# The first loads in one queue, and a second sequence's slots beside the first one's dense mixture

## The chip, the cores and the metric

The kernel runs on one core of a Trainium2 chip. The core has five engines with a sequencer each: PE (matrix products and transposes; PEld is its weight load), DVE, ACT and POOL (element-wise work, POOL also gathers rows by index), and SP, which only issues DMAs. Sixteen DMA engines move data between memory and the on-chip buffers. The metric is the device time of one execution in microseconds (us); less is better. A change of about 0.5% is what runs of this kernel can tell from none.

## The reference, cut to what matters

Eight sequences of 1024 rows of 256 numbers go through three residual blocks: a mixture of experts, an attention block, and the same mixture of experts again.

```python
x = x + 0.5 * ffn(layernorm(x))
x = x + attention(layernorm(x))
x = x + 0.5 * ffn(layernorm(x))

def ffn(y):              # 8 experts of width 128, two of them for each row
    w = softmax(y @ router_w + router_b); keep the two largest, scaled to sum 1
    out = sum over experts e of  w[e] * (gelu(y @ W1[e] + b1[e]) @ W2[e] + b2[e])

def attention(x):
    light: 8 heads of 64 in windows of 64 rows, each with the window before and after
    heavy: two router scores per row; the 256 best rows by each, full attention between them,
           added to the light result at the rows chosen
```

## The kernel before

**Two ways to do a mixture.** Sequence 0's first mixture and sequence 7's last one are *dense* (`dense`): all eight experts for every row, in groups of rows. Per expert, PE makes `ph` (rows turned, 512 columns, two products), ACT takes a Gelu into `act`, PE makes `po` for four tiles of 128 rows, and DVE adds `po` times a row's weight to the rows (`x_0at<-po_0f,weight_0f`, four sums per expert and half). The turned and normalised rows lie in a tile `yTf`. Sequence 0 goes in two halves of four tiles. All other mixtures are *routed*. `rows` normalises a sequence's rows, stores them to memory (`y_1f<-rows_1f`), takes the router's logits (`pl`), ranks the experts (`better`), and gives each pair of row and expert a slot in an order sorted by expert, padded to 128 (`slot`, `at`, and through `who` the `token` of every slot). `experts` then goes through 23 blocks of 128 slots: POOL gathers the rows (`xp`), SP fetches the block's expert, 256.5 KB (`wt<-wpk`, the number read from `te_i`), PE turns the rows (`pt`), makes `ph` and `po`, and the result goes to memory (`ys`). `combine` later gathers a row's two results (`got`) and adds them.

**Packed weights.** `wpk` is a table in memory with one row of w1, w2 and b1 for each expert and partition. Four copies from memory to memory make it at the start; every fetch of `wt` reads it.

**Attention.** `front(b)` adds the gathered results to sequence b's rows (for sequence 0 the dense mixture has done it in place), stores them (`h_a`), normalises, turns them (`xT`), and takes two scores a row (`junk`, `sc`). The scores are turned by PE (`pr`), sent to memory as a line and read back to all partitions (`line`, `rbuf`), and compared with each row's own (`cmp`, 46 DVE steps per sequence) for a `rank`, from which the 256 best rows follow. `project` makes q, k and v into `qT`, `kT` and `v`; `light` and `heavy` are the two attentions.

**What sets the order.** The functions above are generators. They are advanced in the order of a list of stages, `sides`, each with a number of steps and a start and end on an axis on which one sequence is 1 long. An operation is then only recorded. A planner (`Plan`) takes all recorded operations, their data dependencies and the reuse of buffers, estimates costs, and lays out each engine's queue; it does this some rounds, keeps the best by its own estimate, and emits the instructions in that order. An engine runs its queue strictly in order. The recording order decides which buffer of a tag an operation gets, and so which earlier users it must wait for; PSUM banks (three for general use) are given out by the planner. The field `behind` ties an operation to an earlier one in the plan.

**The start.** `nc.sync.dma_start` stands in SP's queue, `nc.scalar.dma_start` in ACT's. In this kernel SP loads all eight tiles of sequence 0's rows in one DMA (1 MB) and then sequence 1's rows. ACT issues the rest: all experts for the dense mixture in two DMAs of 1 MB (`all_experts`), the router, the four copies to `wpk`, the small b2, and the nine attention weights (`attention_loads`); an issuing instruction takes its place in ACT's order among the copies and Gelus. In `sides`, the rows of sequence 1 are recorded from -1.50 to -0.98, its experts from -0.95 to 0.10, and the dense mixture of sequence 0 from -2.2 to -1.6.

Every operation is issued through a recording helper, so the profile gives line 197 for most of them; they are told apart by their tiles' names. In those, `0f` is the first mixture of sequence 0, `7f` that of the last dense one, `1at` the attention of sequence 1, `atl` light and `ath` heavy.

Of the kernel before, what the change touches and what calls it, by code (L numbers as in the profile page):

```python
# [44 lines left out]
F32 = mybir.dt.float32  # L45
# [12 lines left out]
P = 128  # L58
# [158 lines left out]
class Plan:  # L217
# [201 lines left out]
    def schedule(self, before, after, rank):  # L419
# [60 lines left out]
        while len(result) < len(ops):  # L480
            e = min((e for e in ENGINES if found[e]), key=lambda e: found[e][0])
            t, k = found[e]
            o = ops[k]
            for x in o.engines:
                waiting[x].remove((rank[k], k))
            stale = set(o.engines)
            func = o.how.get("func")
            if func in TABLES and func != table:
                t += SWITCH if table else 0
                table = func  # L490
            takes, seen_after = o.cost(e)
            if e == PE:
                changed = o.how["array"] != array
                array = o.how["array"]
                now[e] = run(t, takes + (TURN if changed else 0))
                done = now[e] + (170 if clock[0] == 1 else 230)
            else:
                now[e], done = t + takes, t + seen_after + LATE
            if o.kind == "dma":
                lane = max(t + o.how["lag"] + LATE_DMA - 200, lane) + o.how["bytes"] / RATE  # L500
                done = lane + 300
                length[k] = o.how["lag"] + LATE_DMA + o.how["bytes"] / RATE + 100
            else:
                length[k] = takes + 200 if e == PE else seen_after + LATE
            end = max(end, done)
            result.append((t, k, e))
            for i in self.opens[k]:
                asks[i] -= 1
            for i in self.uses[k]:
                if i not in bank_of:  # L510

                    bank_of[i] = max(
                        free_at,
                        key=lambda x: (free_at[x] <= t, free_at[x] if free_at[x] <= t else -free_at[x], -x),
                    )
                    del free_at[bank_of[i]]
                last_use[i] = max(last_use[i], done)
                left[i] -= 1
                if not left[i]:
                    free_at[bank_of[i]] = last_use[i]  # L520
            if self.opens[k] or self.uses[k]:
                stale.add(PE)
            for q in after[k]:
                missing[q] -= 1
                same = e == PE and ops[q].engines == (PE,)
                ready[q] = max(ready[q], now[e] - SIGNAL[e] if same else done)
                if not missing[q]:
                    for x in ops[q].engines:
                        insort(waiting[x], (rank[q], q))
                        stale.add(x)  # L530
            for x in stale:
                found[x] = next_of(x)
        return end, result, length, bank_of

    def backward(self, before, result, length, bank_of):
# [27 lines left out]
        for _ in range(n):  # L563
            e = min((e for e in ENGINES if found[e]), key=lambda e: found[e][0])
            t, k = found[e]
            waiting[e].remove((-begin[k], -k))
            now[e] = from_end[k] = t + takes[k]
            stale = {e}
            for q in before[k]:
                x = engine[q]  # L570
                if x == PE and e == PE:
                    ready[q] = max(ready[q], from_end[k] + takes[q])
                else:
                    ready[q] = max(ready[q], from_end[k] + length[q] + SIGNAL[e])
                missing[q] -= 1
                if not missing[q]:
                    insort(waiting[x], (-begin[q], -q))
                    stale.add(x)
            for x in stale:
                found[x] = next_of(x)  # L580
# [43 lines left out]
def program(  # L624
# [46 lines left out]


    x1_0 = one.tile([P, NT, D], F32, tag="x1", name="x1_0at")
    nc.sync.dma_start(out=x1_0, in_=by_tile(x, 0))
    b1_sb = load(b1, "b1_sb")

    def all_experts(queue, name):
        t = one.tile([P, 2 * E * D], F32, tag="hbuf", name=name)
        w1_of = t[:, : E * D].rearrange("p (k e h) -> p k e h", k=KD, e=E)
        w2_of = t[:, E * D :].rearrange("p (e d) -> p e d", e=E)  # L680
        queue.dma_start(out=w1_of, in_=w1)
        queue.dma_start(out=w2_of, in_=w2)
        return w1_of, w2_of

    experts_0 = all_experts(nc.scalar, "experts_0")
    rw_sb = load(router_w, "rw_sb")
    rb_sb = cons.tile([P, E], F32, tag="rb_sb", name="rb_sb")
    nc.scalar.dma_start(out=rb_sb, in_=router_b.partition_broadcast(P))
    wpk_p = wpk.rearrange("e p c -> p e c")
    for k in range(KD):  # L690
        nc.scalar.dma_start(out=wpk_p[:, :, ts(k, FE)], in_=w1[:, k, :, :])
    nc.scalar.dma_start(out=wpk_p[:, :, KD * FE : KD * FE + D], in_=w2)
    nc.scalar.dma_start(out=wpk_p[:, :, WROW - 1], in_=b1, allow_slow_non_contiguous=True)

    ident = cons.tile([P, P], F32, tag="ident", name="ident")
    make_identity(nc, ident)
# [69 lines left out]
    expert = cons.tile([96, 1], F32, tag="expert", name="expert")  # L766
    nc.gpsimd.memset(expert, -1.0)
    for i in range(3):
        nc.scalar.dma_start(out=b2_sb[32 * i : 32 * i + E, :], in_=b2)
        nc.gpsimd.iota(  # L770
            expert[32 * i : 32 * i + 32, :],
            pattern=[[0, 1]],
            base=0,
            channel_multiplier=1,
            allow_small_or_imprecise_dtypes=True,
        )

    all_sel = cons.tile([96, E], BF16, tag="all_sel", name="all_sel")
    nc.vector.tensor_scalar(all_sel, place_f[:96, :E], expert, None, op0=ALU.is_equal)
    b2_part = two.tile([P, 2 * D], BF16, tag="y", name="b2_part")[:96, :D]  # L780
    b2_s = cons.tile([96, D], BF16, tag="b2_s", name="b2_s")
    nc.vector.tensor_copy(b2_s, b2_sb)
    for i in range(1, 3):
# [104 lines left out]
    def rows(f, src, group, routed):  # L888
# [12 lines left out]
        for i_b, b in enumerate(group):  # L901
            n = f"{b}f{f}"
            y = one.tile([P, NT, D], F32, tag="rows", name=f"rows_{n}")
            nc.sync.dma_start(out=y, in_=by_tile(src, b)).waits = completed[b] if f else ()
            mv, rstd = yield from stats(y, n)
            ls = lg[:, ts(i_b, NT), :]
            for hf in range(2):
# [240 lines left out]
        nc.vector.tensor_tensor(gate[1], gate[0], ex, op=ALU.mult)  # L1148
        return gate

    def dense(rows_of, weights, n):

# [8 lines left out]
            nc.vector.bn_aggr(mv[:, i, :], st[:, i, :])  # L1163
        nc.vector.tensor_scalar_add(ve[:, :m], mv[:, :m, 1], EPS)
        nc.gpsimd.tensor_tensor(rstd[:, :m], ve[:, :m], mhalf[:, :m], op=ALU.pow)
        yT = one.tile([P, KD, HALF], F32, tag="yTf", name=f"yTf_{n}")
        for h in range(m // 2):
            pt = bank(f"pt_{n}_{h}")
            for i in range(2):
# [624 lines left out]
    def first_dense():  # L1794

        tiles = [x1_0[:, t, :] for t in range(NT)]
        for hf in range(2):
            yield from dense(tiles[4 * hf : 4 * hf + 4], experts_0, f"0f0_{hf}")

    def last_dense(c, last_weights):  # L1800

        if not last_weights:
            last_weights.extend(all_experts(nc.sync, "experts_1"))
        assert ended[0] >= 2 * c + 2
        yield from dense(last_tiles[2 * c : 2 * c + 2], last_weights, f"7f1_{c}")
        for t in (2 * c, 2 * c + 1):
# [35 lines left out]
    def attention_loads():  # L1842

        for t, src in attention_weights:
            nc.scalar.dma_start(out=t, in_=src)
        nc.vector.tensor_scalar_mul(gam16, gam_sb, D**0.5)
        yield

# [4 lines left out]
    sides = []  # L1853
    for group in FIRST:
        a, z = steps(group)
        at = group[0] - 2 + (0.05 if group[0] == 1 else 0)
        sides.append((first_rows(group), a, at - 0.55, at - 0.03))
        sides.append((first_experts(group), z, at, at + 1.05))
    for group in LAST:
# [78 lines left out]
```

## Time and profile before

| | us |
|---|---|
| median of 9 runs | 1851.34 |
| lowest and highest run | 1838.19, 1859.10 |
| the profiled execution: its time | 1845.04 |
| its span in the profile | 1843.3 |
| busy in it: PE, DVE, ACT, POOL | 1698.9, 1351.6, 925.3, 874.8 |
| first 128x512 expert product (ph_0f) starts | 28.41 |
| sequence 0's scores compared (cmp_0at) | 178.3 to 206.2 |
| second sequence's experts' first product (ph_2f) starts | 247.06 |

The profile is of one execution. Its page gives busy times, the span in 40 slices, DMA queues, the chain of work that ended last, and the costliest groups. The trace behind it can be asked for a timeline (start, duration, engine, operation, output and inputs, and in brackets how long the engine was idle before and what released it), for who waited for whom, and for sums over any stretch of time. A DMA's issue stands under the issuing engine with a q.

### The profile page before, as it was taken

Reading aid. Unit: us, or ns where it says so; the run is one execution under the profiler, and the core shown is the slowest. Engines: PE = TensorE matmul, PEld = TensorE weight load, DVE = VectorE, ACT = ScalarE, POOL = GpSimd, SP = SyncE. Lnnn points to the kernel's source line nnn. Section 1 sums busy time; section 2 is a strip of 40 time slices with the busy share of each in tenths; the row PEclk is TensorE's granted clock in tenths of the full one; section 3 lists DMA queues with packets and bytes.
Section 4 is the critical chain, followed back from the end, with each engine's and each line's share of the span. In section 5 each row is a group of like instructions: output and inputs, shape, how many; then the busy total and the mean of one; then the engine's idle time right before and its main releaser. Section 6 shows DMA issues by size and latency. Waiting matters only on the chain.

```text
span 1843.3 us, 40072 instructions
## 1 busy us (share of the span) xinstructions
PE 1698.9 (92%) x13844; PEld 1254.8 (68%) x13844; DVE 1351.6 (73%) x4303; ACT 925.3 (50%) x2568; POOL 874.8 (47%) x771
## 2 busy tenths in 40 slices
PE   4888899999999999899999999999999999899996
PEld 2555577667777677667766777767676777667774
DVE  4563967988795796988993877779774878558744
ACT  1113456545564565446553675646564565555431
POOL 1005363355344671463645555574445635555523
PEclk9988899999999999999999999999999999999998
DMA  8117456234667566245566387555565476535363
GB/s 234 24 59 242 136 178 205 71 115 138 205 220 214 154 198 193 65 138 192 184 188 186 114 255 235 176 169 179 185 197 166 134 233 202 150 109 188 116 190 107
DMA packets 223323, 306.22 MB, mean 166 GB/s; under 512 B 54648, under 2 KB 158736, under 8 KB 221328
## 3 DMA queue, kind: packets, MB, share of 16 engines
q1 hardware_dynamic: 188288, 216.81, 36.8%
q0 software_dynamic: 28608, 78.16, 15.7%
q10 hardware_dynamic: 6224, 8.70, 1.9%
q8 instruction: 109, 1.79, 0.4%
q14 instruction: 94, 0.77, 0.1%
HBM read 214.90 MB, written 83.43 MB: 162 GB/s over the span
## 4 chain that ended last, share of the span: by engine, by line
PE 48%; DVE 22%; DMA 14%; issue 9%; POOL 4%; ACT 3%; POOLq 0%; SPq 0%; ACTq 0%; DVEq 0%
PE po_0f L197 2%; PE ph_0f L197 2%; PE po_7f L197 2%; PE ph_7f L197 1%; DMA xp_5f<-y_5f,token_5f 1%; PE po_1f L197 1%; PE ph_1f L197 1%; PE po_6f L197 1%; DVE cmp_3at L197 1%; DMA wt_6f<-wpk 1%; DVE cmp_1at L197 1%; DMA xp_1f<-y_1f,token_1f 1%; DMA wpk<-in_w 1%; DVE cmp_4at L197 1%; DVE o L197 1%
## 5 line engine op out<-in xcount | busy, mean ns | idle before, releaser
L197 ACT ACT_TABLE_LOAD x93 | 119.3, 1283 | 19.2 <-DVE nmax_6atl L197 8.8
L197 POOL DMA_INDIRECT xp_1f<-y_1f,token_1f x62 | 71.0, 1145 | 72.5 <-PE pt_1f L197 21.4
L197 POOL DMA_INDIRECT xp_3f<-y_3f,token_3f x62 | 65.3, 1053 | 43.8 <-issue 13.9
L197 POOL DMA_INDIRECT xp_6f<-y_6f,token_6f x46 | 48.1, 1046 | 63.2 <-PE pt_6f L197 38.5
L197 POOL DMA_INDIRECT xp_5f<-y_5f,token_5f x46 | 48.0, 1043 | 43.8 <-PE pt_5f L197 23.9
L197 DVE SCALAR_TENSOR_TENSOR x_0at<-po_0f,weight_0f,x_0at 128x256 f32<-128x256 f32 x64 | 27.9, 478 | 39.2 <-PE po_0f L197 38.5
L197 DVE SCALAR_TENSOR_TENSOR x_last<-po_7f,weight_7f,x_last 128x256 f32<-128x256 f32 x64 | 28.2, 479 | 34.6 <-PE po_7f L197 34.4
L197 ACT ACTIVATE act_0f<-ph_0f,b_sb 128x512 f32<-128x512 f32 x16 | 11.0, 687 | 62.1 <-PE ph_0f L197 53.4
L197 PE MATMUL po_0f<-experts,act_0f 128*128 128x256 f32 x128 | 35.8, 386 | 5.3 <-ACT act_0f L197 5.3
L197 POOL DMA_INDIRECT xp_7f<-y_7f,token_7f x23 | 25.2, 1096 | 31.6 <-PE pt_3f L197 15.0
L197 PEld LDWEIGHTS ph_1f<-xTe_1f,wt_1f 128*128 128x128 f32 x248 | 34.4, 194 | 8.3 <-issue 6.6
L197 PE MATMUL ph_3f<-xTe_3f,wt_3f 128*128 128x128 f32 x248 | 37.1, 281 | 2.6 <-DMA wt_3f<-wpk 2.6
L289 POOL TENSOR_TENSOR a_3atl<-a_3atl,asum_3atl 128x768 f32<-128x768 f32 x14 | 20.7, 1481 | 37.7 <-DVE asum_3atl L197 22.9
L197 PEld LDWEIGHTS ph_3f<-xTe_3f,wt_3f 128*128 128x128 f32 x248 | 33.2, 192 | 7.9 <-DMA wt_3f<-wpk 4.5
L289 POOL TENSOR_TENSOR a_2atl<-a_2atl,asum_2atl 128x768 f32<-128x768 f32 x10 | 14.8, 1475 | 48.8 <-DVE asum_2atl L197 27.9
L197 PE MATMUL ph_0f<-yTf_0f,experts 128*128 128x512 f32 x64 | 34.2, 661 | 3.9 <-ACT act_0f L197 3.9
L197 PE MATMUL ph_1f<-xTe_1f,wt_1f 128*128 128x128 f32 x248 | 37.3, 281 | 0.0
L197 PE MATMUL ph_7f<-yTf_7f,experts 128*128 128x256 f32 x128 | 33.6, 385 | 3.6 <-ACT act_7f L197 3.6
L197 POOL DMA_INDIRECT xp_0f<-y_0f,token_0f x23 | 24.2, 1053 | 26.5 <-PE pt_0f L197 12.0
L197 ACT ACTIVATE act_7f<-ph_7f,b_sb 128x256 f32<-128x256 f32 x32 | 15.1, 473 | 42.5 <-PE ph_7f L197 30.6
L197 PE MATMUL po_7f<-experts,act_7f 128*128 128x256 f32 x128 | 36.4, 378 | 0.0
L197 PE MATMUL po_1f<-wt_1f,act_1f 128*128 128x256 f32 x124 | 35.1, 381 | 0.2 <-ACT act_1f L197 0.2
(1570 smaller groups left out, 6197.6 us busy)
## 6 DMA issues: line engine op xcount, KB each, us to landing
wt_1f<-wpk SPq DMA_DIRECT2D x62, 256.5 KB
wt_3f<-wpk SPq DMA_DIRECT2D x62, 256.5 KB
wt_5f<-wpk SPq DMA_DIRECT2D x46, 256.5 KB
wt_6f<-wpk SPq DMA_DIRECT2D x46, 256.5 KB
ys_1f<-yp_1f SPq DMA_DIRECT2D x30, 256.0 KB
ys_3f<-yp_3f SPq DMA_DIRECT2D x30, 256.0 KB
o<-h_b SPq DMA_DIRECT2D x56, 128.0 KB
out_x<-o SPq DMA_DIRECT2D x56, 128.0 KB
```

The lines of the kernel that those rows point to most:

```text
L197: op = Op(self.plan, engines, lambda _: issue(*args, **kw), outs, ins, kind, **how)
L289: return getattr(nc, engine).tensor_tensor(dst, dst, by, op=ALU.mult)
```

## The change

- The loads of the start go through `in_line` into SP's queue, one behind the other in the plan: two tiles of sequence 0's rows, two more, the first four experts in three DMAs, the other four tiles, the other four experts, sequence 1's rows, b2, the copies to `wpk`, the nine attention weights. ACT keeps b1 and the router's two.
- `all_experts` loads in six DMAs, four experts at a time, with the layout of w1 in its tile unchanged in size.
- The planner treats an operation that is `behind` a DMA as able to follow at once, without waiting for the DMA's end.
- Sequence 1's rows are recorded from -2.15 to -1.7 and its experts from -1.3 to -0.3. The first half and second half of sequence 0's turned rows lie in `qT`, so that the tile `yTf` is free for sequence 1's.
- `b2_part` takes another buffer.

The planner lays out the whole program anew, so queues differ in detail from there to the end.

```diff
@@ schedule
-                same = e == PE and ops[q].engines == (PE,)
+                same = e == PE and ops[q].engines == (PE,) or ops[q].behind is o and o.kind == "dma"
@@ backward
-                if x == PE and e == PE:
+                if x == PE and e == PE or self.ops[k].behind is self.ops[q] and self.ops[q].kind == "dma":
@@ program, the first loads
-    nc.sync.dma_start(out=x1_0, in_=by_tile(x, 0))
+    first_loads = []
+
+    def in_line(out, in_, **kw):
+
+        o = nc.sync.dma_start(out=out, in_=in_, **kw)
+        o.behind = first_loads[-1] if first_loads else None
+        first_loads.append(o)
+
+    def load_x1_0(t):
+        in_line(x1_0[:, t : t + 2, :], by_tile(x, 0)[:, t : t + 2, :])
+
+    for t in range(0, 4, 2):
+        load_x1_0(t)
     b1_sb = load(b1, "b1_sb")
-    def all_experts(queue, name):
+    def all_experts(name, dma_start, between=None):
         t = one.tile([P, 2 * E * D], F32, tag="hbuf", name=name)
-        w1_of = t[:, : E * D].rearrange("p (k e h) -> p k e h", k=KD, e=E)
-        w2_of = t[:, E * D :].rearrange("p (e d) -> p e d", e=E)
-        queue.dma_start(out=w1_of, in_=w1)
-        queue.dma_start(out=w2_of, in_=w2)
+        w1_of, w2_of = t[:, : E * D], t[:, E * D :]
+        w1_of = w1_of.rearrange("p (e k h) -> p k e h", k=KD, e=E)
+        w2_of = w2_of.rearrange("p (e d) -> p e d", e=E)
+        for e in range(0, E, 4):
+            for k in range(KD):
+                dma_start(out=w1_of[:, k, e : e + 4, :], in_=w1[:, k, e : e + 4, :])
+            dma_start(out=w2_of[:, e : e + 4, :], in_=w2[:, e : e + 4, :])
+            if between and not e:
+                for t in range(4, NT, 2):
+                    between(t)
         return w1_of, w2_of
-    experts_0 = all_experts(nc.scalar, "experts_0")
+    experts_0 = all_experts("experts_0", in_line, load_x1_0)
...
     for k in range(KD):
-        nc.scalar.dma_start(out=wpk_p[:, :, ts(k, FE)], in_=w1[:, k, :, :])
-    nc.scalar.dma_start(out=wpk_p[:, :, KD * FE : KD * FE + D], in_=w2)
-    nc.scalar.dma_start(out=wpk_p[:, :, WROW - 1], in_=b1, allow_slow_non_contiguous=True)
+        in_line(wpk_p[:, :, ts(k, FE)], w1[:, k, :, :])
+    in_line(wpk_p[:, :, KD * FE : KD * FE + D], w2)
+    in_line(wpk_p[:, :, WROW - 1], b1, allow_slow_non_contiguous=True)
...
-        nc.scalar.dma_start(out=b2_sb[32 * i : 32 * i + E, :], in_=b2)
+        nc.sync.dma_start(out=b2_sb[32 * i : 32 * i + E, :], in_=b2).behind = first_loads[4]
...
-    b2_part = two.tile([P, 2 * D], BF16, tag="y", name="b2_part")[:96, :D]
+    b2_part = two.tile([P, 2 * D], BF16, tag="hrow", name="b2_part")[:96, :D]
@@ rows
-            nc.sync.dma_start(out=y, in_=by_tile(src, b)).waits = completed[b] if f else ()
+            asked = nc.sync.dma_start(out=y, in_=by_tile(src, b))
+            asked.waits = completed[b] if f else ()
+            asked.behind = first_loads[9] if group == FIRST[0] and not f else None
@@ dense
-    def dense(rows_of, weights, n):
+    def dense(rows_of, weights, n, yT=None):
...
-        yT = one.tile([P, KD, HALF], F32, tag="yTf", name=f"yTf_{n}")
+        if yT is None:
+            yT = one.tile([P, KD, HALF], F32, tag="yTf", name=f"yTf_{n}")
@@ first_dense
-            yield from dense(tiles[4 * hf : 4 * hf + 4], experts_0, f"0f0_{hf}")
+            yT = qT[:, :KD, ts(hf, HALF)]
+            yield from dense(tiles[4 * hf : 4 * hf + 4], experts_0, f"0f0_{hf}", yT)
@@ last_dense
-            last_weights.extend(all_experts(nc.sync, "experts_1"))
+            last_weights.extend(all_experts("experts_1", nc.sync.dma_start))
@@ attention_loads
-            nc.scalar.dma_start(out=t, in_=src)
+            in_line(t, src)
@@ sides
-        at = group[0] - 2 + (0.05 if group[0] == 1 else 0)
+        at = group[0] - 2
+        if group == FIRST[0]:
+
+            sides.append((first_rows(group), a, -2.15, -1.7))
+            sides.append((first_experts(group), z, -1.3, -0.3))
+            continue
```

## The prediction

> **What bounds the kernel now.** First the page: TensorE is busy for 92% of the span, so time can be won only where it is idle or slow. Its 40 slices say that this is at the front.
>
> ```profile
> span 1843.3 us, 40072 instructions
> ...
> PE 1698.9 (92%) x13844; PEld 1254.8 (68%) x13844; DVE 1351.6 (73%) x4303; ACT 925.3 (50%) x2568; POOL 874.8 (47%) x771
> ...
> PE   4888899999999999899999999999999999899996
> ```
>
> Then a table by stage, cut where the work changes (stretch, its length, PE, PEld, DVE, ACT and POOL busy, granted clock, DMA share, GB/s):
>
> ```profile
> 0.00:25.00 25.00, 2.52 (x9) 1.29 (x9) 13.07 (x56) 1.95 (x3) 6.56 (x26) 1.00 1.00 266
> 25.00:40.00 15.00, 12.79 (x29) 6.52 (x30) 5.15 (x24) 3.06 (x4) 1.01 (x1) 1.00 0.91 272
> 40.00:72.00 32.00, 29.35 (x137) 18.97 (x135) 15.65 (x37) 4.71 (x7) 0.00 (x0) 1.00 0.20 36
> 72.00:111.00 39.00, 34.68 (x146) 20.66 (x145) 18.79 (x58) 6.58 (x10) 1.01 (x1) 1.00 0.00 1
> 111.00:120.00 9.00, 4.57 (x41) 4.25 (x39) 6.66 (x23) 1.07 (x2) 3.27 (x2) 0.80 0.80 255
> 120.00:145.00 25.00, 23.11 (x78) 11.21 (x78) 24.43 (x127) 6.38 (x11) 7.64 (x3) 0.87 0.22 66
> 145.00:151.00 6.00, 0.03 (x1) 0.06 (x1) 0.00 (x0) 0.00 (x0) 4.51 (x5) 0.67 0.94 279
> ...
> 206.00:247.00 41.00, 31.71 (x208) 23.35 (x207) 36.05 (x158) 16.50 (x50) 22.89 (x21) 0.83 0.48 148
> ...
> 400.00:1800.00 1400.00, 1332.18 (x11493) 1002.46 (x11492) 1051.60 (x3251) 768.59 (x2167) 719.43 (x619) 0.99 0.58 176
> ```
>
> PE is idle 22.5 us before 25, 4.4 in 111:120, 6.0 in 145:151 and 9.3 in 206:247; after 400 only 68 us in 1400. DVE has half of 40:111 free and is full in 120:145. Two orderings cause the holes, as the timeline shows (start, us, engine, operation, idle time and its releaser):
>
> ```profile
> 23.04 1.28 ACT L280 ACT_TABLE_LOAD   x1 [23.04 <-issue]
> 24.33 1.07 ACT L280 COPY yTf_0f<-pt_0f 128x512 f32<-128x512 f32 x2
> 30.96 0.58 ACTq L197 DMA_DIRECT2D wpk<-in_w  x1
> 31.57 1.28 ACT L197 ACT_TABLE_LOAD   x1 [6.16 <-DMA wpk<-in_w]
> 32.86 0.69 ACT L197 ACTIVATE act_0f<-ph_0f,b_sb 128x512 f32<-128x512 f32 x1
> ```
>
> ```profile
> 28.41 3.76 PE L197 MATMUL ph_0f<-yTf_0f,experts 128*128 128x512 f32 x4
> 33.60 3.78 PE L197 MATMUL ph_0f<-yTf_0f,experts 128*128 128x512 f32 x4 [1.44 <-ACT act_0f L197]
> ```
>
> ```profile
> 150.97 0.66 PE L197 MATMUL pt_1f<-ident,xp_1f 128*128 128x128 f32 x2 [6.94 <-DMA xp_1f<-y_1f,token_1f]
> ...
> 157.79 0.27 PE L197 MATMUL pr_0at<-ident,sc_0at 128*16 128x128 f32 x1
> ```
>
> ACT issues 18 loads before its first copy, and holds its first Gelu behind one more. Later sequence 1's slots come out of a full DVE at 136, PE waits for the gathered rows until 151, and the scores of sequence 0 (pr_0at) stand behind them in PE's order. Their DMA round trip (line_0at, rbuf_0at) ends when the comparisons cmp_0at start, at 178.3; they end at 206.2, and the second sequence's first expert product (ph_2f) runs at 247.1.
>
> **The change part by part**, against the profiled execution (span 1843.3, 1845.0 with what lies around it; the runs' median is 6.3 higher).
>
> 1. First loads. ACT keeps three small ones. SP asks for 0.5 MB of x, then half the experts (1 MB). SP's queue alone moved 318 GB/s in 115:120, so 0.5 MB takes 1.7 us and 1.5 MB 4.9; about 2.9 us of round trip (the 8 KB line_1at took 2.86) and two issues of 0.45 put the four tiles at 5.5 and the weights at 9. From first BN to last y, row by row: 4 BN 1.4, aggregates and ve 0.5, POOL's power 1.1, four y 1.5; transposes and copy 1.3; pl 3.5 at the slow rate that 24.97 shows. Less 0.3, by which pl may start on the first copy, the first ph stands at 14.5 instead of 28.4: **-13.9**. SP's 27 issues of 0.33 to 0.6 us lie beside transfers. The slow first experts stay: 28.41 to 40.15 is kept as it is.
>
> The queue's length is new. Some 10.7 MB stand before y_1f: at the first slice's 234 GB/s that is 46 us, at 318 GB/s 34. I take 46, as the copies to wpk are the same. y_1f (1 MB) lands at 52, and only then may rows_2f load into the same tile: 58. DVE reaches st_2f, after 28 of the half's 32 sums, at about 54. In-order DVE then holds the last sums and PE's banks: **+3** (0 to 6).
>
> The Trainium skill ("DMA: Bandwidth & Descriptors", Specifications) says transfers under 512 B miss line rate; the 4-byte column of wpk now heads the attention weights in that queue. The stretch 55:57 has a DMA share of 0.54 for 25 GB/s, which agrees. The same page's HBM limit of 358 GB/s would end the queue near 32 us and take the +3 off.
>
> 2. Sequence 1's rows beside the dense mixture. Into its first half come 16 pt_1f (0.11 each) and 16 pl_1f (0.21): 5.1 us, into PE gaps of 0.4 an expert: **+2.5**. Half two takes the places and who of sequence 1 and the rows of 2. Between the halves DVE needed 6.6 us from the last sum to weight_0f (72.1 to 78.7), while PE needed until 80.2. Now there are 20 small steps of slot arithmetic (0.18) 3.6, 7 BN (0.34) 2.4 and 8 rows_2f (0.38) 3.0 more, 15.6 in all; and 16 spot comparisons (0.18) with 4 tiled products (0.27), 4 us, stand among the next sums. PE goes on with three banks and two act tiles, and loses of these 8 + 4 us about **+4** (2 to 8). q's tile costs nothing: project writes qT after the mixture. Dense end: 111 - 13.9 + 3 + 2.5 + 4 = 106.5, and about 9 us of PE work that stood behind 111 is done.
>
> 3. What follows. Gathers and six weight blocks are there at 106.5, so the holes 111:120 and 145:151 close. Up to sequence 1's last po PE has 66 us: 23 slots of ph (0.45) and po (1.09 a pair), 42 products of project (0.86), 62 transposes; with 4 us of small waits, 177. Scores reach PE at 106.5+25; rbuf_0at stands on SP behind the weights of slot 21, which need slot 15's buffer (33 us of PE work), so it is asked for at 143, lands at 151 (8 us, between 4.8 for rbuf_1at and 12 for rbuf_0at), and cmp_0at ends 28 us later, at **179** (before: 206.2).
>
> Here a wait takes its place. In the built program x_1at, the sum of sequence 1's gathered results, now stands in DVE's order straight behind rank_0at, ahead of the tokens. It needs every ys_1f in memory: 177 + 0.6 copy + 3 store + 1.1 issue + 4 gather = 186. DVE stands 7 us; behind it stand best_i_0at, the places of sequence 2, and so POOL's gathers and PE. Then before's own stretch: 206.2 to 235.7 for DVE (28.4 of 29.6 busy) and 11.4 to ph_2f. 186 + 29.5 + 11.4 = 227, against 247.1: **-20**. PE has by then done 4 us more (pt_3f, pl_3f), DVE 6 us more (st_3f, rows_3f): **-7**, between the two and both (4 to 10), since 320 to 400 is as full on DVE (77.5 of 80) as on PE. Without the wait it would be -27 and -7; with rows_2f on time and quick banks, -42.
>
> The sum is **-27** for 1818 on the profile's terms. From 250 on the order differs in detail, but first ph_3f, pc_0f and pz_6at stand within 6 us of the same PE work. In the median's terms 1851.3 - 27 = **1824**.
>
> The Trainium skill ("TensorE: Matmul & The Clock Gate", What's actually happening) gives half rate after an idle window of about 3.4 us. The clock of 0.67 in 145:151 agrees. By that page the 7 us wait on DVE could slow PE again, 3 us more; the kept stretch 206:247 already holds a clock of 0.83.
>
> **The rivals.**
> - A: as summed, with the waits for rows_2f and x_1at: 1807 to 1833.
> - B: neither wait bites. For: DVE is only half busy in 40:111. Against: both stand in DVE's order. 1851 - 42 = 1809, down to 1800.
> - C: the slots part comes back as DVE waits and only the start's 14 remain: 1837. For: 206:247 is DVE's already (36 of 41).
> - D, slower: the single queue is slow. The stretch 20:25 moved 97 GB/s at a share of 1.19; at that rate the 12.8 MB up to rows_2f take until 132, 78 us after DVE wants them, of which 4 are summed: 1851 - 27 + 74 = 1898. It decides when they land after 85, an average under 155 GB/s. Against: 266 and 272 GB/s in 0:40 with the same copies.
> - E: the new order loses later what it won. 400:1800 idles 4.9%; at 6.8% the 27 us are gone: 1851, 1843 to 1860.
>
> **How the numbers follow.** A 0.48, B 0.20, C 0.15, D 0.06, E 0.11. About 0.5% is what these runs can tell, so faster means under 1842: A, B and nearly all of C, 0.82. Same is most of E: 0.08. Slower is D and the rest of E: 0.10. The range runs from B's end, 1800, to C with a small loss, 1844; A's own is 1807 to 1833.
>
> **What would show it.** First ph_0f at 13 to 17 and ACT without the 23 us of issue; st_2f waiting for rows_2f near 54; the last sum of x_0at near 106; no wait of PE for xp_1f; cmp_0at from about 151; x_1at waiting for got_1at for some 7 us; ph_2f near 227. Wrong I would be if experts arrive late (ph_0f after 20), if the mixture grows by over 15 us, if ph_2f is past 240, or if PE's idle share after 400 leaves 4 to 6%.

## The result, and the profile after

The changed kernel takes **1859.78 us** (median of 17 runs, 1849.3 to 1870.02); the kernel before, measured beside it, 1846.55. The ratio is 1.0078, with a 95% interval of 1.0059 to 1.0096: slower by 13 us, where 1824 us and a gain of 27 had been forecast. The ratios below are all to the kernel before on the same chip in the same group of runs; in two groups (one with p1_loads, one with r1_after_again) every kernel took 5 to 6% longer, before included (1939.6 and 1954.8 us), so numbers are compared within a group only.

Three lines of the page of the changed kernel; in the last one each digit is PE's busy share in a fortieth of the span:

```profile
span 1861.2 us, 40023 instructions
...
PE 1711.6 (92%) x13844; PEld 1266.3 (68%) x13844; DVE 1355.9 (73%) x4300; ACT 930.1 (50%) x2579; POOL 874.2 (47%) x765
...
PE   5999789899999988899899999998899999999996
```

The first digits are better than the 4888 of before. The loss is not at one place. To see it, PE's work was followed through both traces: each kind of matmul is counted with its mean time in the trace of before, and the *lead* at a time t is how much earlier than t the other kernel had done as much as before has at t (minus means ahead). This is worked out, not read off, and wrong by a few us where the two orders run different kinds.

| at, us | 50 | 100 | 200 | 250 | 400 | 600 | 800 | 900 | 1350 | 1800 |
|---|---|---|---|---|---|---|---|---|---|---|
| after | -17 | -6 | -21 | -10 | -8 | -7 | +13 | +18 | +25 | +19 |

So 17 us are won, 11 of them lost between 50 and 100, nearly all in one step near 54; 15 more are won until 200, and 11 lost by 250. Then nothing happens for 350 us, and between 600 and 1350 a further 32 us go. The table by stage of the changed kernel (stretch, its length, PE, PEld, DVE, ACT and POOL busy, granted clock, DMA share, GB/s) has the same places:

```profile
0.00:25.00 25.00, 14.32 (x43) 8.23 (x44) 15.46 (x69) 5.11 (x6) 5.84 (x26) 1.00 1.00 211
25.00:50.00 25.00, 12.39 (x62) 8.41 (x60) 9.59 (x29) 2.46 (x4) 1.64 (x1) 0.79 0.93 188
...
150.00:175.00 25.00, 25.00 (x101) 14.64 (x100) 12.77 (x45) 11.48 (x26) 0.00 (x0) 1.00 0.61 219
175.00:200.00 25.00, 20.37 (x94) 10.70 (x92) 20.36 (x84) 11.58 (x29) 6.44 (x6) 0.93 0.12 37
200.00:225.00 25.00, 19.30 (x89) 15.71 (x90) 20.27 (x92) 3.44 (x8) 13.99 (x11) 0.53 0.19 53
...
400.00:1800.00 1400.00, 1316.57 (x11324) 989.21 (x11323) 1043.93 (x3200) 755.87 (x2133) 707.68 (x604) 0.98 0.57 172
```

PE stands for half of 25:50; it runs at a clock of 0.53 in 200:225; and from 400 to 1800 it idles 83 us instead of 68, and at a clock that is a hundredth lower. Of the 27 us of lead lost in that long stretch, 16 are idle time and the rest is slower running.

**The first loss is a DMA that the prediction did not look at.** PE's and then DVE's timeline of the changed kernel (start, us, engine, operation, and in brackets the idle time with its releaser):

```profile
14.68 3.76 PE L197 MATMUL ph_0f<-qT,experts 128*128 128x512 f32 x4
...
35.55 1.02 PE L197 MATMUL ph_0f<-qT,experts 128*128 128x512 f32 x2
49.01 3.58 PE L197 MATMUL pl_1f<-rw_sb,yTf_1f 128*128 128x8 f32 x16 [12.43 <-DVE x_0at L197]
```

```profile
34.34 0.88 DVE L197 SCALAR_TENSOR_TENSOR x_0at<-po_0f,weight_0f,x_0at 128x256 f32<-128x256 f32 x2 [1.45 <-PE po_0f L197]
48.00 0.17 DVE L197 TENSOR_SCALAR gam<-gam_sb 128x2 f32<-128x2 f32 x1 [12.78 <-DMA gam_sb<-in_gamma_h]
48.08 0.88 DVE L197 SCALAR_TENSOR_TENSOR x_0at<-po_0f,weight_0f,x_0at 128x256 f32<-128x256 f32 x2
```

PE waits for a sum (x_0at) that is ready to run, but stands in DVE's order behind gam16, the scaling of 256 numbers that only the attention needs, sequence 0's first. Its operand gam_sb stands near the end of SP's new line. In before it was asked for at 15.71 on ACT's queue, and gam did not wait:

```profile
15.71 0.45 ACTq L197 DMA_DIRECT2D gam_sb<-in_gamma_h  x1
...
31.83 0.16 DVE L197 TENSOR_SCALAR gam<-gam_sb 128x2 f32<-128x2 f32 x1
```

Issues of the new line on SP:

```profile
14.39 2.61 SPq L197 DMA_DIRECT2D wpk<-in_w  x1
17.05 8.06 SPq L197 DMA_DIRECT2D wpk<-in_b  x1
25.16 5.88 SPq L197 DMA_DIRECT2D lng_sb<-in_ln_g  x1
31.08 2.00 SPq L197 DMA_DIRECT2D lnb_sb<-in_ln_b  x1
...
36.76 1.43 SPq L197 DMA_DIRECT2D gam_sb<-in_gamma_h  x1
```

The issues themselves are held for 8.06 and 5.88 us, and the table in 6 us steps (columns as above) says why the line is late:

```profile
12.00:18.00 6.00, 6.00 (x18) 3.83 (x17) 3.71 (x15) 1.52 (x2) 1.01 (x1) 1.00 1.14 293
18.00:24.00 6.00, 4.44 (x11) 1.65 (x11) 4.71 (x24) 1.37 (x2) 1.01 (x1) 1.00 1.24 96
24.00:30.00 6.00, 6.00 (x35) 4.38 (x34) 5.86 (x24) 0.69 (x1) 1.64 (x1) 1.00 1.04 93
30.00:36.00 6.00, 5.82 (x29) 3.74 (x27) 3.77 (x11) 1.43 (x3) 0.00 (x0) 1.00 0.90 112
...
42.00:48.00 6.00, 0.00 (x0) 0.00 (x0) 0.00 (x0) 0.00 (x0) 0.00 (x0) 0.50 0.78 292
```

For 18 us (18:36) the DMA engines are full and move a third of the 293 GB/s ahead of it: here the copies into wpk, its column of 4-byte pieces and the two columns of 8 bytes a partition pass. Which of these fills the engines can be summed from the packets of the trace: of 305 us that the packets starting in 18:36 took on the sixteen engines, 278 are those of 512 and 1024 bytes, which are the copies of w1 and w2, and 11 those of 4 and 8 bytes. Their size alone is not what makes them slow: a 512-byte piece of the experts' load took 31 ns on the mean in 9:12, one of the copy from memory to memory 114 to 140 ns in 18:27. Behind them the big attention weights pass, and the 128 pieces of gam_sb come only in 45:48. Before had the same rate while one such copy passed (the last three columns are clock, DMA share and GB/s):

```profile
18.00:24.00 6.00, 0.72 (x3) 0.29 (x2) 3.66 (x18) 0.96 (x1) 1.64 (x1) 1.00 1.26 103
```

The **second** loss is in 186:206. Two lines of the list of PE's waits there name it (waited for, us in total, times, longest):

```profile
PE pw_0at L197 <- DVE tiled_0at L197: 4.3, 1, 4.3
PE pb_0atl L197 <- DVE a_0atl L289: 2.8, 1, 2.8
```

The work that filled this place in before, sequence 1's slots, is already done, so PE waits bare for the choice of sequence 0; then comes the clock of 0.53. The Trainium skill ("TensorE: Matmul & The Clock Gate", What's actually happening) has the array's clock halved after about 3.4 us without work; the gap of 4.3 us and the clock of 0.50 in 42:48 agree with it in the main; by the trace the clock fell a little sooner, at 39.3 us behind a last matmul that ended at 36.57.

### The profile page after: what moved, and what is told of

Same layout as the page of the kernel before. It is cut to its first block, busy times and chain, and to the rows that moved or that the text cites. A ratio compares the mean times of both kernels' runs of the same rounds, so it can differ in the third digit from the quotient of the medians.

```text
span 1861.2 us, 40023 instructions
## 1 busy us (share of the span) xinstructions
PE 1711.6 (92%) x13844; PEld 1266.3 (68%) x13844; DVE 1355.9 (73%) x4300; ACT 930.1 (50%) x2579; POOL 874.2 (47%) x765
## 4 chain that ended last, share of the span: by engine, by line
PE 49%; DVE 23%; DMA 15%; issue 6%; POOL 3%; ACT 2%; SPq 2%; POOLq 0%; DVEq 0%; ACTq 0%
PE po_7f L197 2%; PE ph_7f L197 2%; PE po_0f L197 2%; SPq L197 2%; PE ph_0f L197 1%; PE po_3f L197 1%; PE po_1f L197 1%; PE ph_1f L197 1%; DVE cmp_2at L197 1%; DVE cmp_3at L197 1%; PE po_6f L197 1%; DVE cmp_1at L197 1%; PE ph_3f L197 1%; DMA xp_5f<-y_5f,token_5f 1%; DVE cmp_4at L197 1%
## 5 line engine op out<-in xcount | busy, mean ns | idle before, releaser
L197 POOL DMA_INDIRECT xp_3f<-y_3f,token_3f x62 | 69.6, 1122 | 56.2 <-PE pt_3f L197 20.4
L197 POOL DMA_INDIRECT xp_1f<-y_1f,token_1f x62 | 66.0, 1065 | 58.7 <-PE pt_1f L197 31.4
L197 POOL DMA_INDIRECT got_1at<-ys_1f,at_1f x16 | 18.3, 1141 | 59.1 <-DMA ys_1f<-yp_1f 43.5
L289 POOL TENSOR_TENSOR a_1atl<-a_1atl,asum_1atl 128x768 f32<-128x768 f32 x10 | 14.9, 1493 | 49.3 <-DVE asum_1atl L197 24.7
L197 PE MATMUL ph_0f<-qT,experts 128*128 128x512 f32 x64 | 34.3, 654 | 2.8 <-ACT act_0f L197 2.8
L197 PE MATMUL po_3f<-wt_3f,act_3f 128*128 128x256 f32 x124 | 36.4, 391 | 0.1
```

What stands on the lines that cost most here:

```text
L197: op = Op(self.plan, engines, lambda _: issue(*args, **kw), outs, ins, kind, **how)
L289: return getattr(nc, engine).tensor_tensor(dst, dst, by, op=ALU.mult)
```

## The experiments

Two theories were tested. **Theory 1**: gam's wait ate what the first loads won. **Theory 2**: what is lost behind 470 us belongs to the new order alone, which a planner made from the same work; an order is fixed for every engine, so another order of the same operations would keep the lead. Against the second stands that the lead cannot be kept in any order, because something else than the order bounds the long stretch.

To join two orders, the kernels with a *tail* or a *cut* make both plans and take the first up to one PSUM tile, and what is left in the order and on the engines of the other:

```diff
-        order = draft.order()
+        order = joined(draft, draft.order(), other, other.order())
...
+def joined(a, order_a, b, order_b):
+    at = next(j for j, (k, _) in enumerate(order_a) if k in a.users[cut])
+    head = order_a[:at]
+    place = {b.key[k]: (j, e) for j, (k, e) in enumerate(order_b)}
...
+    waiting = sorted(rest, key=lambda k: place[a.key[k]][0])
+    # one by one: the first in this order whose operands and PSUM bank are there
```

An operation's key is its stage and its number within the stage. The joined kernels also load the weights of the last dense part in two DMAs, as before does; the changed kernel asks for these weights only at 1679 us, so they bear on nothing that differs earlier.

### The first group: the line of loads, and two joined orders

**e1_gam**, the load of gam_sb meant for ACT's queue:

> The kernel after with its written-out order unchanged, but the load of gam_sb is issued first of all on ACT's queue instead of 25th in SP's line. Nothing is left out. Theory 1 (the wait for gam on VectorE ate what the first loads won): gam16 runs without its 12.8 us wait, pl_1f comes at about 37 instead of 49.0, PE from 25 to 50 is busy more than 20 of 25 us instead of 12.4, the landmarks that follow come 8 to 12 us earlier (last weight of the dense part at about 106), and since every engine's order is fixed the gain is carried: 1848 to 1852 us against 1859.8 of the change, that is a ratio to before of about 1.001 to 1.003. Rival (something else than gam holds the start: the matrix of the dense part is limited by the sums or the loads anyway, or the gathers of sequence 1 set the end of this stretch): pl_1f moves, but the first slots' experts (ph_1f at 115.7, sim_0atl at 191.7) move under 3 us and the time stays at 1857 to 1862.

Measured: 1855.87 us, 1.0074 (1.0045 to 1.0103). The edit did not take hold: SP still issued gam_sb, at 34.16 us, so this run is the changed kernel once more and says only that 1.0078 repeats.

**e1_col**, the 4-byte column at the end of the line:

```diff
+            column = [x for x in order if self.ops[x[0]].how.get("column")]
+            order = [x for x in order if x not in column]
+            at = order.index(last[0]) + 1
+            for k, e in order[:at] + column + order[at:]:
```

> The kernel after with its written-out order unchanged, but the DMA that writes the one column of wpk from b1 is issued behind the attention weights instead of ahead of them. Nothing is left out. If this DMA of 4-byte pieces holds the issuing queue (8.06 us between its issue and the next in the profile of after), gam_sb is issued about 8 us earlier (at about 29 instead of 36.8) and lands at about 40 instead of 48.0; the wait of gam16 falls from 12.8 to about 5 us and the time by 4 to 8 us, to 1852 to 1856. If the 8 us are the ring or the engines of DMA being full of the weights before it, whatever DMA stands there, gam_sb is issued no earlier than 35 and the time stays within 2 us of 1859.8.

Measured: 1855.08 us, 1.0056 (1.0022 to 1.0089). Its 6 us table, and DVE's gam:

```profile
18.00:24.00 6.00, 4.44 (x6) 1.47 (x6) 5.72 (x33) 1.38 (x2) 1.39 (x2) 1.00 1.23 109
24.00:30.00 6.00, 6.00 (x30) 3.97 (x29) 3.18 (x9) 0.69 (x1) 1.25 (x1) 1.00 1.16 116
30.00:36.00 6.00, 5.82 (x28) 3.82 (x27) 4.43 (x13) 1.19 (x2) 0.00 (x0) 1.00 0.99 218
```

```profile
43.33 0.17 DVE L197 TENSOR_SCALAR gam<-gam_sb 128x2 f32<-128x2 f32 x1 [6.60 <-DMA gam_sb<-in_gamma_h]
```

gam_sb is issued at 27.09 instead of 36.76 (29 was forecast), and its wait falls from 12.78 to 6.60 us (5); but it lands at 43.3, 16 us after its issue, and lng_sb, now in the column's place, is held 6.65 us. So the column holds part of the line (the slow stretch ends about 6 us sooner), and the hold is not its own: whatever comes behind the copies into wpk waits. The end moved by 0.2% against e1_gam, inside both intervals, so the 4 to 8 us that had been expected are not shown.

**e2_tail_before** and **e3_tail_after**, the two orders joined at pc_0f both ways:

> Two plans joined: the order of the kernel after up to the first use of pc_0f (456.9 us in its profile), from there on what is left in the order in which the kernel before has it, engines chosen as there. The loads are those of after, but the weights of the last dense part come in two DMAs as before. Nothing is left out. Theory 2 (the 15 us won until 457 are lost in the new order of the rest, whose work is the same): the gain of 14.8 us at pc_0f stays to the end, so 1846.6 - 15 = about 1832 (1827 to 1838), a ratio of about 0.992 to before, and PE from 600 to 800 is as busy as in before (95 of 100 us instead of 89 and 90). Rival (what is won early cannot be kept: the later stretch is bound by something that the early finish doesn't advance, such as weights from memory, VectorE, or the clock): 1845 to 1860, with pz_3at and pz_4at no earlier than in before.

> The reverse: loads and order of the kernel before up to the first use of pc_0f (471.7 us in its profile), from there on what is left in the order of the kernel after. Nothing is left out. Theory 2: the front costs what it costs in before and the rest loses what it loses in after, some 33 us between 470 and 1010: about 1846.6 + 31 = 1878 (1868 to 1886). Rival (the rest's order is as good as before's, and the loss belongs to the front of after, through what it leaves behind): 1840 to 1850, as before.

Measured: after's front with before's rest 1840.15 us, 0.998 (0.996 to 1.0); before's front with after's rest 1878.78, 1.0182 (1.0154 to 1.0209). Against the changed kernel in the same group (e1_gam) before's rest saves 16 us, and 36 us lie between before's front with its own rest and with after's. The lead of e2 is 12 to 16 from 400 to 550 and 7 at the end; e3 has none at 400 and is 36 behind at 1800, as expected. At 1350, ahead of the last dense weights, e2 leads by 7 and e1_gam is 22 behind. That after's order of the rest is the dearer one, whichever front it follows, by 16 us and by 36, is shown; that the front's gain is kept in full is not, as half of e2's lead goes. 0.992 had been expected, 0.998 came.

### The second group: gam again, and each part alone

**e4_gam_early** and **e5_gam_early_tail_before**:

```diff
+            early = [k for k, _ in order if self.ops[k].how.get("early")]
+            for k, e in [(k, ACT) for k in early] + [x for x in order if x[0] not in early]:
...
+        if out.name.startswith("gam_sb"):
+            o.how["early"] = True
+            o.call = lambda e: getattr(nc.nc, e).dma_start(out=out, in_=in_, **kw)
```

> The kernel after with its written-out order unchanged, and the load of gam_sb as the first issue on ACT's queue instead of 25th in SP's line (in the earlier run of this idea gam_sb was still issued by SP, at 34.16 us, so that run was the kernel after once more: 1.0074). Nothing is left out. Theory 1: gam16's wait (11 to 12.8 us) goes, pl_1f comes at about 35 to 38, PE from 25 to 50 is busy 20 of 25 us or more, and the lead over before, which falls from 16 us at 50 to 5 to 7 us at 100, stays at 14 or more; the end comes 6 to 11 us earlier than in after, a ratio to before of 1.001 to 1.004. Rival (the next thing in the same line, the loads or the sums of sequence 1, holds PE as long): pl_1f no earlier than 43, as with the column moved, ratio 1.005 to 1.008. A third outcome, that the early part gains 8 us and the hole at 193 to 206 us (pw_0at waiting for the choice of sequence 0) takes them back, shows as ph_1f 6 to 9 us earlier and pw_1at as before.

> gam_sb first on ACT's queue, after's order up to the first use of pc_0f, from there on what is left in before's order. Nothing is left out. The run with before's order behind pc_0f gave 0.998 with 11 us of lead at pc_0f, of which 7 were left at the end. If gam's 8 to 11 us are carried: lead at pc_0f 17 to 22 us, end 1846.6 less 12 to 18, a ratio of 0.990 to 0.994. If the hole at 193 to 206 us takes them: 0.996 to 1.000.

Measured: 1.0101 (1.0061 to 1.0141) and 0.994 (0.9907 to 0.9972). In e4 gam no longer waits, pl_1f starts at 36.57 instead of 49.0, and PE is busy 24.48 of 25:50 at a clock of 1.00, as expected; the ratio did not follow. In this group the changed kernel itself was not run, and in the next one it came out at 1.0173, so e4 says nothing on gam's worth at the end. Its third reading stays undecided too: beside the first profile of the changed kernel ph_1f comes 5.6 us earlier and pw_1at no earlier (341.4 and 340.7), beside that of r1_after_again 6.4 and 11 us earlier. Between e4 and e5, which differ in the rest's order and the two DMAs of the last weights, lie 32 us; e5 came at the upper end of its first reading.

**p1_loads** and **p2_sides**, each part alone, planned anew:

> Part 1 of the change alone: the first loads in SP's line, the stages' places, yTf and b2_part as in before, and the whole order planned anew. Nothing is left out. ph_0f at about 14.5 as in after. If the loads by themselves are sound and a new plan by itself costs nothing: the start's 13 us less what gam's wait takes (0 to 12), 1834 to 1846, a ratio of 0.993 to 1.000. If any new plan of the long rest costs what it cost in after (theory 2, 16 to 33 us between 470 and 1010): 1850 to 1868, a ratio of 1.003 to 1.012.

> Part 2 of the change alone: sequence 1's rows and first slots recorded beside the dense part, its turned rows in qT, b2_part in hrow's place; the loads on their queues as in before, the whole order planned anew. Nothing is left out. ph_0f at 28 as in before; the first slots' experts before the attention of sequence 0. If the moved stage alone wins what it showed in after between 100 and 200 us (lead from 5 to 20 us): a lead of about 10 to 15 us at 200 and of 0 to 8 at 250, and with no cost of a new plan 1838 to 1848. If a new plan costs what it did in after: 1855 to 1875.

Measured: 1.0089 (1.0056 to 1.0121) and 1.0004 (0.9973 to 1.0036). The loads alone come out slower although ph_0f starts at 18.5 instead of 28.4 (14.5 was expected), as theory 2 would have it; their gam waits 10.50 us. The stages alone come out even, although they lead by 17 us at 200 and by 10 at 250, more than expected. But the changed kernel's own ratio differs by 1% between groups (1.0074 and 1.0173), so these two, from a group in which it did not run, are not to be read finer than that and decide nothing by themselves.

### The third group: where to cut

> The changed kernel itself once more, on the chip on which the three others of this group run, so that they have it beside them. 1.006 to 1.0095 to before, as measured first (1.0078) and once more (1.0074).

> Part 1 alone (loads in SP's line), in the order that was planned for it only up to the first use of pt_1f at 103 us; from there on what is left in before's order. The weights of the last dense part come in two DMAs as before. Nothing is left out. Part 1 planned anew throughout gave 1.0089 although it led by 12.6 us at 50 and by 4 at 100. If the new order of the rest is what made it slow: the 4 us of lead stay, 0.996 to 0.999. If the loads in one line harm something later by themselves: above 1.004.

> gam_sb first on ACT's queue, after's order only up to the first use of pw_0at (194 us, a lead of 24 us over before in the run with gam_sb early), from there on before's order. Nothing is left out. The run that kept after's order to 457 us gave 0.994, and its lead fell from 25 at 200 to 15 at 250. If after's order in 200 to 250 is what loses these 10 us: 0.986 to 0.990. If they are lost because the experts of sequence 1, which filled this place in before, are already done, then in any order: 0.992 to 0.997.

> The same with the cut at the first use of pr_0at (141 us, lead 17 us), so that the choice of sequence 0, its projections and the second half of sequence 1's experts stand in before's order. Nothing is left out. If the hole at 193 to 206 us comes from after's order between 141 and 198: lead kept, 0.988 to 0.992. If it comes from the cover that is used up: 0.993 to 0.999.

Measured: the changed kernel 1.0173 (1.0145 to 1.0201), far above what it had given twice; part 1 with before's order behind 103 us 1.0011 (0.9989 to 1.0033), between its two readings and 0.8% better than the same part planned throughout, though in another group; cut at 198, 0.9919 (0.9896 to 0.9942); cut at 141, **0.9887** (0.9859 to 0.9915). The cut at 198, with after's order kept up to the hole at 193 to 206, came out at the lower edge of its second reading; the cut at 141, which gives that hole another order ahead of it, came out where its first reading had it. The two intervals overlap, so the place of the cut is worth some 0.3%, likely and not certain. The leads of the fourth group carry it further: with the cut at 141 and gam in line, 3 us are lost between 200 and 250, where after loses 11.

### The fourth group: is it the stages or the draw, and what is gam worth

```diff
-LATE, LATE_DMA = 150, 500
+LATE, LATE_DMA = 150, 480
```

The number is a lag of a DMA, in ns, in the planner's estimates. It reaches the chip only through the plan: the order, the PSUM banks, and which engine takes some of the operations (DVE has 4300 instructions in the changed kernel, 4321 when planned with 480 and 4330 with 520).

> The kernel before, planned with a DMA lag of 480 ns in the planner's estimates instead of 500: another order, no other change. Nothing is left out. If any new plan moves the time by as much as the change did: more than 0.5% from 1.000, to either side (before's own order may be a lucky one, then 1.005 to 1.015). If plans of the same stages are alike, and after's loss belongs to its stages' places: 0.997 to 1.003.

> The kernel after, planned with 480 ns instead of 500: another order of the same stages. Nothing is left out. If the loss is the order's: more than 0.5% away from after's 1.007 to 1.017, in either direction. If it belongs to the stages' places: 1.006 to 1.018 again.

> The kernel before, planned with a DMA lag of 520 ns in the planner's estimates instead of 500. Nothing is left out. If orders of one and the same work spread by about 1%, as the first two did: 0.995 to 1.015, and more likely above 1 than below, since before's own order is the better of the two seen.

> The kernel after, planned with 520 ns instead of 500. Nothing is left out. If after's stages are the better ones by some 10 us and its own order was a poor draw: 0.990 to 1.000. If 0.9944 was the lucky draw: 1.004 to 1.015.

> gam_sb first on ACT's queue, after's order up to the first use of pr_0at, then before's order, once more beside the run without gam's early load. Nothing is left out. 0.986 to 0.991 to before, as the first time (0.9887).

> The same kernel with gam_sb in SP's line as in after. If gam's wait (11 to 12.8 us on VectorE, 8 us of PE's lead at 100 us) is carried to the end in a sound order: 0.4 to 0.6% above the run with gam early, 0.992 to 0.996. If what follows takes it back: within 0.2% of it.

| kernel | planned with 480 | with 500 (as it is) | with 520 |
|---|---|---|---|
| before | 1.0055 (1.0027 to 1.0082) | 1 | 1.0012 (0.9989 to 1.0035) |
| after | **0.9944** (0.9915 to 0.9972) | 1.0078 (1.0059 to 1.0096) | 1.0208 (1.0163 to 1.0253) |

One and the same changed kernel is 0.6% faster or 2.1% slower than before, by 20 ns in an estimate; 1.0208 lies above both readings written down for it. The leads say where (us, minus is ahead; after_480 and after_520 are the two new orders of the changed kernel):

| at, us | 100 | 250 | 400 | 600 | 800 | 900 | 1350 | 1800 |
|---|---|---|---|---|---|---|---|---|
| after | -6 | -10 | -8 | -7 | +13 | +18 | +25 | +19 |
| after_480 | -7 | -14 | -11 | -7 | -2 | +2 | +4 | -1 |
| after_520 | -9 | -12 | -11 | -11 | -7 | +2 | +18 | +24 |
| e7, gam early | -14 | -22 | -23 | -23 | -22 | -23 | -21 | -20 |
| e7, gam in line | -6 | -13 | -13 | -13 | -11 | -9 | -5 | -7 |

Up to 600 the three orders of after are within 5 us of one another, with the gam wait in all of them; then each loses at its own place, after between 600 and 900 (after_480 loses 9 there), after_520 between 800 and 1350. PE in 600:900, for after, after_480 and before in turn:

```profile
600.00:900.00 300.00, 274.30 (x2334) 202.84 (x2333) 235.26 (x729) 159.02 (x458) 151.73 (x122) 0.97 0.48 147
```

```profile
600.00:900.00 300.00, 283.28 (x2393) 210.26 (x2393) 241.14 (x737) 157.32 (x456) 157.89 (x131) 0.96 0.50 151
```

```profile
600.00:900.00 300.00, 284.33 (x2567) 210.50 (x2566) 245.27 (x757) 163.42 (x485) 152.29 (x126) 0.99 0.50 155
```

After idles 25.7 us there, the others 16.7 and 15.7, and no other engine is full meanwhile. Its waits are many and small (PE's list of waits in 600:910 for after):

```profile
PE sim_2atl L197 <- DVE cmp_3at L197: 3.7, 1, 3.7
PE pt_1f L197 <- DMA xp_1f<-y_1f,token_1f: 3.2, 2, 1.8
PE ph_4f L197 <- DMA wt_4f<-wpk: 2.3, 1, 2.3
PE sim_2atl L197 <- DVE sim_2atl L197: 2.0, 3, 0.9
```

The two kernels cut at 141 keep their lead from 250 to the end within 3 us (gam early) and 8 us (in line): 1824.1 us, 0.9867 (0.9822 to 0.9911), and 1832.5, 0.9903 (0.987 to 0.9936). The intervals of the two overlap, so the 0.4% that gam is worth at the end is the expected size and not shown by the ratios alone. Run against run, without the runs of before that both share, the means differ by 7.8 us with a standard error of 2.6, which makes it likely; their profiles show it from the start. PE's pl_1f and DVE's gam with gam early:

```profile
40.38 1.85 PE L197 MATMUL pl_1f<-rw_sb,yTf_1f 128*128 128x8 f32 x16
```

```profile
39.10 0.16 DVE L197 TENSOR_SCALAR gam<-gam_sb 128x2 f32<-128x2 f32 x1
```

and in line:

```profile
48.85 3.58 PE L197 MATMUL pl_1f<-rw_sb,yTf_1f 128*128 128x8 f32 x16 [11.52 <-DVE x_0at L197]
```

```profile
47.84 0.17 DVE L197 TENSOR_SCALAR gam<-gam_sb 128x2 f32<-128x2 f32 x1 [11.88 <-DMA gam_sb<-in_gamma_h]
```

Theory 1 stands for the front: 8.5 us of pl_1f, and 8 of the lead at 100. Theory 2 stands for the long stretch, with one addition: before's order is not better than after's by nature; each order is a draw.

The kernel with gam early and the cut at 141 beats both the kernel before and the changed one; it was the fastest in both groups in which it ran.

## Why the prediction was wrong

- **The start (-13.9, ph_0f at 14.5): right.** 14.68, at the front of a lead of 17 at 50.
- **"SP's 27 issues of 0.33 to 0.6 us lie beside transfers", and +3 for the queue's length: the first step that failed.** The length of the line was priced for one of its customers, rows_2f, for which DVE never waited. The customer that hurt was gam_sb, in the same line, with a reader that DVE reaches at 35.2 and that waits until 48.0. In place of +3 (0 to 6) the lead fell by some 11. It could have been seen: for every DMA moved into the line, the question is when its first reader comes up in that engine's order. The working also took 234 GB/s throughout, "as the copies to wpk are the same": a misreading, since that is the rate of before's first 46 us, and two of its four copies were asked for only at 48.53 and 53.30. The 18 us at 93 to 112 GB/s are what rival D had spoken of (97 GB/s), and it is the copies that fill them, not the 4-byte column that the prediction looked at. D had the mechanism and the wrong victim, and its point of decision, rows_2f after 85, never came.
- **Rows and slots beside the dense part (+2.5, +4): the right kind of cost, too small.** The dense part ended at 116.9, where 106.5 was forecast (its terms add up to 106.6). 8 of the 10 us between are gam's: in the pair cut at 141 it ended at 109.4 with gam early and at 117.5 with gam in line. With gam early, and the +3 not called for, the end at 112.0 in before and the 13.5 us won at the start leave 10.8 us for the two terms, where 6.5 (4.5 to 10.5) were summed.
- **The holes 111:120 and 145:151: right, they closed.** PE is full in 150:175.
- **x_1at behind rank_0at, 7 us of DVE: the place right, the cause not.** POOL's gather got_1at did stand 43.5 us until 190.15, but x_1at did not wait for it there: DVE stood 4.49 us for PE's sim_0atl before it, and PE then waited for DVE (4.3 and 2.8). cmp_0at ended at 188.8 (179 forecast) and ph_2f came at 241.5 (227), 5 us more than gam explains.
- **The clock behind that hole: mis-sized.** The prediction left it out of its sum and gave 3 us as what the skill's page would add; PE ran at a mean of 0.53 for 25 us. The lead fell by 10.7 there, hole and clock together.
- **-27 at 250: 10 were there.** With gam early and before's order behind 141, 22 were. That this kernel takes 1824.1 us, the number forecast for the change, is in part luck: it is another kernel, and it shows that the mechanism of the front was nearly right, not that the forecast was. Of the 45 us between the forecast -27 and the +18 of the two profiled executions, 20 are missing at 600 and 26 more go between there and 1800.
- **Rival E, "the new order loses later what it won": what happened, at a chance of 0.11.** It was priced at 6.8% idle after 400, 1843 to 1860; PE idled 6.0%, ran a little slower, and the time was 1859.8. The failed step behind this is "from 250 on the order differs in detail, but first ph_3f, pc_0f and pz_6at stand within 6 us of the same PE work": equal PE work ahead of a landmark says nothing of the waits between. The orders of before spread over 0.55% and those of after over 2.6%, three of each; a gain of 27 us (1.5%) was forecast as though such a draw were worth nothing.

Open stays why the changed kernel came out at 1.0173 in the third group, against 1.0074 and 1.0078; its instructions have the same median durations there (a pav matmul 267 ns in both), while the gaps between PE's instructions grow from 128 to 198 us, and PE's busy time from 1711.6 to 1759.4 at a mean clock of 0.957 instead of 0.971. And three orders of each kernel do not tell whether the changed stages, on the whole, are better, even or worse.

## What to carry to other kernels

When loads are put into one line, list for each the first instruction that reads it and where that stands in its engine's order; a reader of a few numbers, early in an in-order queue, stops an engine as surely as the big ones. Where a planner orders the work, a change at the front redraws the whole order behind it: plan it several times with estimates that differ by nothing that matters, or keep the old order for what was not changed, before a difference of 1 or 2% is put down to the change. A change whose gain lies at the front should be carried by joining its front to the old order, which here, with gam's load moved, gained 1.1 and 1.3% in two groups, where the change alone cost 0.8%.

## What was not expected of the hardware

DMA engines that are full can be moving a third of their rate: 93 to 112 GB/s at a share of 0.90 to 1.24 in 18:36, behind 293 GB/s in 12:18, while copies from memory to memory in pieces of 512 and 1024 bytes pass, with pieces of 4 and 8 bytes among them; by the packets it is the copies that take the engines' time (278 of 305 us, against 11). SP is then held at its next issues for 8.06 and 5.88 us, and the hold passes to the next DMA when the one that stood there is moved (6.65 us for lng_sb). gam_sb as the first issue on ACT's queue, at 0.80 us, was there before DVE asked for it; whether the other queue or the early place did it, these runs do not tell apart.
